# A Macaron block (top-k feed-forward, selective scan, feed-forward): the transposed gate moved from TensorE to VectorE and DRAM, softplus from one table, and a new issue order

## The chip, the cores and the metric

One core of one Trainium2 chip. The metric is the device time of one execution in microseconds (us), median of several runs. Five engines run their own instruction queues in order: PE (TensorE, matmuls), DVE (VectorE), ACT (ScalarE), POOL (GpSimd) and SP (SyncE, which in this kernel issues all DMAs). An instruction that waits on a semaphore holds everything behind it in its queue.

## The reference

`x` is [2, 2048, 1024] in float32. The block applies a feed-forward, a selective scan and the same feed-forward again:

```
x = x + 0.5 * ffn(layernorm(x))
x = x + ssm(layernorm(x))
x = x + 0.5 * ffn(layernorm(x))

ffn(x):  vecs   = A x                      # 64 experts a, rank 16 r
         arrows = norm(vecs over r)        # one number for each expert
         routes = one_hot(top4(arrows)).sum / 4
         v      = sum_a routes[a] vecs[a, r]
         return x W^T + bias + sum_{a, r} routes[a] v[r] B[a, :, r]

ssm(x):  delta_r, B, C = split(x Wx^T)
         delta = softplus(delta_r Wdt^T + b_dt)
         h_t   = exp(-delta exp(A_log)) h_{t-1} + delta B x      # 1024 channels, 16 states each
         return sum_n(h C) + x D
```

The last term of the feed-forward is a matrix product g B', where g[token, (r, a)] = v[token, r] * routes[token, a]. As the left operand of a matmul it is needed transposed, with (r, a) on the partitions: g^T.

## The kernel before, in words

The 4096 tokens are worked in 16 chunks of 256, two tiles of 128 tokens each. Each tile goes through the first feed-forward ("f"), a chunk then through the projections and softplus (`prepare`) and the scan (`scans`), and each tile through the second feed-forward ("g"). So there are 64 feed-forward tiles. For each, PE does three products of [128 x 1024] by [1024 x 1024]: `wa` (vecs), `ww` (x W^T) and `wb` (g B'). All three are issued at L578, 16 matmuls each, which the profile shows as 32 records since one float32 matmul is two.

Between the end of `wa` and the start of `wb` of the same tile lies the route chain: ACT squares vecs into `g` (`square`, L631); DVE sums the squares for each expert (L645), takes the top values (L648), marks them (L649) and turns the marks into 0.25 or 0 (L652); DVE multiplies vecs by the routes (`routed`, L658) and sums them into v (L668); POOL multiplies v by the routes into g (`spread`, L677, two halves); PE transposes g in eight blocks of 128 x 128 (`turn`, L560), ACT copies each half from PSUM to `gt` (L565), and `wb` reads `gt`. While that chain runs, PE works on `ww` of the same tile, which doesn't need it.

The scan keeps the channels replicated over partitions: SP fetches `rep` (delta and delta x, replicated 8 times by a broadcast read) from `du_d` in DRAM (L890), ACT makes the decay with Exp (L917), DVE makes the entry (L925) and scans (L932, two for each step), ACT saves the last state (L942), POOL multiplies by C (L945) and joins halves (L964), PE sums over states (L974), DVE adds the skip term (L988) and turns the result (L991), and SP stores and refetches it (`y_d`, `yt`, L385).

Softplus in `prepare` is made of six steps for each half of a chunk: ACT takes Abs and Relu of z + b (L806, L807), Exp of -|z| (L819), DVE three operations (L822, L827, L830), ACT Ln (L833), DVE one more (L836). Exp and Ln load different tables (ACT_TABLE_LOAD).

The order on every queue is not the order of the source. Each piece of work is a `Task` with an engine, a cost in us, a rank, the buffers that it takes and gives, and the tasks that it waits for. `Plan.order` runs a list schedule over these (an engine that is free takes the ready task of lowest rank whose buffers are free), and the instructions are emitted in the order of their planned starts. Costs, the latency from one engine to another (`HOP`) and the time in which a DMA lands stand in the `add` calls. The PSUM pool `bank` has five banks; `g`, `gt` have one buffer, `xnt` two, `rep` four.

Of the kernel before, what the change touches and what calls it, by code (L numbers as in the profile page):

```python
# [9 lines left out]
FP = mybir.dt.float32  # L30
AF = mybir.ActivationFunctionType
# [20 lines left out]

class Place:
# [10 lines left out]
class Task:  # L64
    __slots__ = (
        "eng", "cost", "emit", "rank", "take", "give", "port", "land", "turn", "waits", "users", "n",
        "at",
# [9 lines left out]
class Plan:  # L77
# [3 lines left out]
    HOP = 0.14  # L81
# [11 lines left out]
    def add(  # L93
        self, eng, cost, emit, reads=(), writes=(), rank=0.0, take=(), give=(), port=False, land=0.0,
        turn=None,
    ):
        t = Task()
        t.eng, t.cost, t.emit, t.rank = eng, cost, emit, rank
# [27 lines left out]
    def order(self):  # L126
# [7 lines left out]
        now = 0.0  # L134

        def arrive(t):
            heapq.heappush(ready[t.eng], (t.rank() if callable(t.rank) else t.rank, t.n))
# [5 lines left out]
        while True:  # L143
            moved = True
            while moved:
                moved = False
                for e in self.ENGINES:
# [34 lines left out]
                    end = now + t.cost  # L182
                    busy[e] = end
# [4 lines left out]
                    heapq.heappush(events, (end, t.n, 0))  # L188
# [7 lines left out]
            if kind == 0:  # L196
                if t.land:
                    heapq.heappush(events, (now + t.land, n, 1))
                else:
                    kind = 1  # L200
            if kind == 1:
# [4 lines left out]
                for u in t.users:  # L206
                    v = tasks[u]
                    v.waits -= 1
                    if v.waits == 0:
                        if v.eng == t.eng and not t.land:  # L210
                            arrive(v)
                        else:
                            heapq.heappush(events, (now + self.HOP, u, 2))
# [13 lines left out]
def macaron_kernel(  # L227
# [54 lines left out]
    places("stats", 6, [P, 17])  # L282
    places("choice", 2, [P, NA + len(PADS) + RANK])
# [4 lines left out]
    plan.pool("du_d", [dram.tile([D, 2, TC], FP, name=f"du_d{j}") for j in range(6)])  # L288
# [32 lines left out]
    pads = const.tile([P, len(PADS) + 1], FP, name="pads")  # L321
    less = pads[:, len(PADS) :]
    nc.gpsimd.memset(less, -1.5)
    for j, v in enumerate(PADS):
        nc.gpsimd.memset(pads[:, j : j + 1], v)

    marked = []
    for j in range(2):
        norms = const.tile([P, NA + len(PADS)], FP, name=f"norms_{j}")
        nc.gpsimd.tensor_copy(norms[:, NA:], pads[:, : len(PADS)])  # L330
        tops = const.tile([P, 2, 8], FP, name=f"tops_{j}")
        nc.gpsimd.tensor_copy(tops[:, 1, :TOPK], pads[:, :TOPK])
        marked.append((norms, tops))
    plan.pool("marked", marked)
# [10 lines left out]
    def load_rows(c, i):  # L345
# [16 lines left out]
        if c == 0:  # L362
            add("SP", 0.4, load_t, [], [(xt, 0), (xt, 1)], rank=-125.7 * n - 1008.5 if n else -2000.0,
                take=[xt], land=1.8)
            add("SP", 0.4, load, [], row(x_p), rank=121.5 * n - 1006.8, take=[x_p], land=1.4)
        else:
            add("SP", 0.8, emit, [], [(x_p, q) for q in range(KC)] + [(xt, 0), (xt, 1)],
                rank=n - (1006.5 if c == 1 else 100.0), take=[x_p, xt], land=5.5)

    def load_sum(c, i, rank):  # L370
# [5 lines left out]
        for g in range(2):  # L376
            yt = Place("yt")

            def fetch(g=g, yt=yt):
# [13 lines left out]
                take=[yt] if g else [x_p, yt], give=[y_d, x1_d], land=7.2)  # L393
# [13 lines left out]
    def load_all():  # L407
        def one(dst, src, key, us, rank):
            keys = [(*key, h) for h in range(2)] if isinstance(key, tuple) else [key]
            add("SP", us, lambda: nc.sync.dma_start(out=dst, in_=src), [], keys, rank=rank, land=3.6)  # L410

        def big(w_sb, w, name, rank):
# [10 lines left out]
            rank=-1000.0, take=[mean_w])  # L423
# [17 lines left out]
        for w_sb, name, key in ((wa, "wa", "pv"), (ww, "ww", "po")):  # L441
            total = Place("row" if name == "wa" else "delta")
            for k in range(1, KC):
                def gather(k=k, w_sb=w_sb, total=total):
# [5 lines left out]
                    take=[total] if k == 1 else [], port=True)  # L450
# [17 lines left out]
            for h in range(2):  # L468
# [10 lines left out]
                for k in range(KC):  # L479
# [4 lines left out]
                    add("DVE", 0.49, center, [(pt, 0)], [(name, k, h)], rank=-900.0, give=[pt])  # L484
# [6 lines left out]
            [], ["half_bias"], rank=272.6)  # L491
# [15 lines left out]
    def spread_of(x_p, st, factor, rank, after=()):  # L507
# [21 lines left out]
        def root():  # L529
            hv, r, t, q = (st.tile[:, j : j + 1] for j in (14, 15, 16, 12))  # L530
# [5 lines left out]
        add("DVE", 1.95, stats, row(x_p) + list(after), [(st, 0)], rank=-109.8 + rank, take=[st])  # L536
        add("ACT", 2.64, root, [(st, 0)], [(st, 1)], rank=72.4 + rank)

    def normalize(x_p, xn_p, rank, after=()):
# [4 lines left out]
        def scale():  # L544
            r, s = st.tile[:, 15:16], st.tile[:, 16:17]
# [6 lines left out]
    def turn(src, keys, dst, out_keys, rank, take=(), give_src=None):  # L552

        for g in range(2):
# [9 lines left out]
            def act(g=g, pt=pt):  # L564
# [4 lines left out]
                give=[src] if give_src else [])  # L569
# [510 lines left out]
```

## Time and profile before

| | us |
|---|---|
| median of 3 runs | 3112.06 (3110.25 to 3116.23) |
| span of the profiled execution | 3105.1 |
| PE busy | 3054.2 |
| ACT busy | 1869.4 |
| POOL busy | 2364.5 |
| mean granted TensorE clock | 0.998 |
| 16 DMA engines, share of the span that the dynamic queue's packets took | 52.6% |

The profile page comes from one execution. It gives for each engine the time in which it was busy, and for groups of equal instructions their count, total and mean time, the engine's idle time just before them and what ended that. Ends of matmuls are modelled, so the issue interval (from one start to the next, 0.432 us for a 128x512 float32 record) is the better measure of what a matmul costs. A window table gives the busy time by stretches of the span, a timeline the instructions in order of time.

### The profile page before, as it was taken

To read this page: it belongs to the slowest core of one execution; us is meant where nothing else is said; L and a number is where in the kernel's file an instruction comes from. 1 tells how busy PE (TensorE), PEld (TensorE's weight loads), DVE (VectorE), ACT (ScalarE), POOL (GpSimd) and SP (SyncE) were. 2 spreads that over 40 slices of the span, in tenths; PEclk is the share of its full clock that TensorE was granted. 3 is DMA by queue.
4 is the path that set the end of the run, shared out by engine and by line. 5 is a ranking of instruction groups with operands and counts; after the bars stand their busy time and mean duration, and the time that the engine had idled before them with its cause. 6 is when DMAs were issued, how large, how long until landed. Compare 5 with 4: busy or idle time off the path is not lost.

```text
span 3105.1 us, 36153 instructions
## 1 busy us (share of the span) xinstructions
PE 3054.2 (98%) x9020; PEld 1409.4 (45%) x9020; DVE 2816.7 (91%) x4683; ACT 1869.4 (60%) x4851; POOL 2364.5 (76%) x1882
## 2 busy tenths in 40 slices
PE   8999999999999999999999999999999999999999
PEld 3444444444444444444444444444444444444444
DVE  4279999999999999999999999999999999997951
ACT  1366666656666676666566665666557675565531
POOL 3148787888788788788887887878888788886861
PEclk9999999999999999999999999999999999999999
DMA  5154654646465465555555555555465555544630
GB/s 226 61 167 147 194 146 138 195 142 190 130 183 157 145 181 163 154 159 163 166 172 150 165 162 164 166 166 169 133 172 168 166 161 148 160 143 130 170 81 14
DMA packets 408371, 478.69 MB, mean 154 GB/s; under 512 B 161504, under 2 KB 253280, under 8 KB 408160
## 3 DMA queue, kind: packets, MB, share of 16 engines
q1 hardware_dynamic: 408160, 476.37, 52.6%
q8 instruction: 72, 1.18, 0.2%
q14 instruction: 139, 1.14, 0.1%
HBM read 375.07 MB, written 101.19 MB: 153 GB/s over the span
## 4 chain that ended last, share of the span: by engine, by line
PE 60%; DVE 24%; issue 6%; ACT 4%; DMA 2%; POOL 2%; SPq 0%; DVEq 0%; POOLq 0%; ACTq 0%
PE bank L578 53%; DVE h L932 10%; DVE h L925 5%; PE bank L974 2%; PE bank L560 2%; PE bank L748 1%; POOL h L945 1%; DVE g L658 1%; ACT da L917 1%; DVE norms L645 1%; PE bank L797 1%; DVE stats L512 1%; DMA rep<-du_d 1%; DVE choice L652 1%; DVE bank L988 1%
## 5 line engine op out<-in xcount | busy, mean ns | idle before, releaser
L945 POOL TENSOR_TENSOR h<-h,c 128x512 f32<-128x512 f32 x1024 | 1323.7, 1303 | 351.8 <-ACT state L942 316.8
L917 ACT ACTIVATE da<-rep,a_neg 128x256 f32<-128x256 f32 x2048 | 974.8, 477 | 725.4 <-DVE h L932 675.6
L932 DVE TENSOR_TENSOR_SCAN h<-da,state,h 128x256 f32<-128x256 f32 x2048 | 1404.8, 731 | 7.3 <-ACT da L917 5.5
L578 PE MATMUL bank<-wa,xnt 128*128 128x512 f32 x2048 | 905.6, 596 | 5.4 <-DVE wa L482 4.0
L578 PE MATMUL bank<-wb,gt 128*128 128x512 f32 x2048 | 895.9, 595 | 10.0 <-ACT gt L565 9.8
L578 PE MATMUL bank<-ww,xnt 128*128 128x512 f32 x2048 | 889.4, 592 | 0.0
L964 POOL TENSOR_TENSOR h<-h,h 128x512 f32<-128x512 f32 x512 | 654.7, 1279 | 40.1
L925 DVE TENSOR_TENSOR h<-rep,b 128x512 f32<-128x512 f32 x1024 | 670.2, 665 | 12.5 <-ACT b L879 6.7
L578 PEld LDWEIGHTS bank<-ww,xnt 128*128 128x128 f32 x2048 | 389.1, 190 | 489.8 <-issue 483.4
L578 PEld LDWEIGHTS bank<-wb,gt 128*128 128x128 f32 x2048 | 384.4, 190 | 485.2 <-issue 453.5
L578 PEld LDWEIGHTS bank<-wa,xnt 128*128 128x128 f32 x2048 | 384.9, 191 | 483.4 <-issue 470.8
L677 POOL TENSOR_TENSOR g<-choice 128x512 f32<-128x512 f32 x128 | 143.5, 1142 | 195.8 <-DVE choice L668 195.8
L942 ACT COPY state<-h 128x2 f32<-128x2 f32 x1024 | 187.9, 185 | 54.5 <-DVE h L932 53.3
L631 ACT ACTIVATE g<-bank 128x512 f32<-128x512 f32 x128 | 133.8, 1047 | 87.9 <-PE bank L578 55.6
L512 DVE BATCH_NORM_STATS2 stats<-xf 128x6 f32<-128x512 f32 x128 | 81.2, 676 | 57.4 <-DMA xf<-in_x 57.4
L616 POOL TENSOR_TENSOR xf<-xf,half_bias 128x512 f32<-128x512 f32 x64 | 81.1, 1287 | 66.4 <-DVE stats L512 66.3
L974 PE MATMUL bank<-h,summer 128*32 128x512 f32 x1024 | 123.1, 598 | 0.0
L645 DVE TENSOR_REDUCE norms<-g 128x64 f32<-128x1024 f32 x64 | 77.0, 1203 | 50.8 <-ACT g L631 49.4
L533 ACT ACTIVATE stats<-stats,pads 128x1 f32<-128x1 f32 x288 | 111.3, 387 | 9.7
L565 ACT COPY gt<-bank 128x512 f32<-128x512 f32 x128 | 71.4, 592 | 66.9 <-PE bank L560 66.4
L695 DVE SCALAR_TENSOR_TENSOR xg<-bank,stats,xg 128x512 f32<-128x512 f32 x64 | 47.4, 741 | 67.6 <-PE bank L578 67.2
L532 ACT ACTIVATE stats<-stats 128x1 f32<-128x1 f32 x288 | 58.1, 202 | 81.8 <-DVE stats L527 75.7
(84 smaller groups left out, 1969.2 us busy)
## 6 DMA issues: line engine op xcount, KB each, us to landing
rep<-du_d SPq DMA_DIRECT2D x1024, 256.0 KB, 3.7
xnt<-in_x_t SPq DMA_DIRECT2D x32, 512.0 KB, 4.1
xf<-in_x SPq DMA_DIRECT2D x32, 512.0 KB, 5.4
x_d<-xf SPq DMA_DIRECT2D x32, 512.0 KB, 3.3
u_d<-u SPq DMA_DIRECT2D x32, 512.0 KB, 4.7
ysb<-u_d SPq DMA_DIRECT2D x64, 256.0 KB, 3.4
du_d<-delta SPq DMA_DIRECT2D x32, 512.0 KB, 3.2
du_d<-u SPq DMA_DIRECT2D x32, 512.0 KB, 3.5
```

What stands on the lines that cost most here:

```text
L512: nc.vector.bn_stats(st.tile[:, 6 * s : 6 * s + 6], x_p.tile[:, s * HD : (s + 1) * HD])
L533: nc.scalar.activation(t, q, AF.Identity, bias=less, scale=hv)
L578: nc.tensor.matmul(ps[h].tile, lhsT=lhs.tile[:, k, :], rhs=w[:, k, h * HD : (h + 1) * HD], start=start and k == 0, stop=stop and k == KC - 1,)
L631: nc.scalar.activation(g_p.tile.rearrange("p (a r) -> p r a", r=RANK)[:, h * r2 : (h + 1) * r2, :], vecs(pv, h), AF.Square,)
L677: nc.gpsimd.tensor_mul(g_p.tile[:, h * HD : (h + 1) * HD].rearrange("p (r a) -> p r a", a=na), ch.tile[:, :NA].unsqueeze(1).to_broadcast([ ...
L917: nc.scalar.activation(da.tile[:, k, :], r.tile[:, k, 0, :], AF.Exp, scale=a_neg[:, q + k, j, hi : hi + 1],)
L925: nc.vector.tensor_mul(h.tile, r.tile[:, :, 1, :], bs[hi].tile.unsqueeze(1).to_broadcast([P, 2, TC]),)
L932: nc.vector.tensor_tensor_scan(h.tile[:, k, :], da.tile[:, k, :], h.tile[:, k, :], state[:, q + k, j, hi : hi + 1], ALU.mult, ALU.add,)
L942: nc.scalar.copy(state[:, q : q + 2, j, hi : hi + 1], h.tile[:, :, TC - 1 : TC])
L945: nc.gpsimd.tensor_mul(h.tile, h.tile, cs[hi].tile.unsqueeze(1).to_broadcast([P, 2, TC]))
L964: nc.gpsimd.tensor_add(first.tile, first.tile, h.tile)
L974: nc.tensor.matmul(y.tile[j // 2 * 2 * DB : (j // 2 + 1) * 2 * DB, :], lhsT=summer[:, DB * (1 - j % 2) : DB * (3 - j % 2)], rhs=sums[j].ti ...
```

## The change

Six things at once.

1. g is no longer formed in the token-major layout and transposed. DVE writes the 64 routes and the 16 sums v into one tile `rv` [128 x 96], turns it in 32 x 32 blocks (`transpose`), and SP writes it to DRAM as `rv_d` [96 x 128] with four DMAs (`put_rv`, runs of 128 bytes). SP then fetches it with four more (`fetch_rv`): the routes twice into `rt` [128 x 128], and the sums as rows of 4 KB, each broadcast to 64 partitions, into `gt`. POOL multiplies `gt` by `rt` in place (`spread`). The transposes on PE and the copies on ACT for g are gone. The columns of `wa` are laid out in another order on the host to suit.
2. The marks become 0.25 or 0 in one ACT instruction (`mark`, Relu with scale -0.25 and bias -1) in place of one on DVE.
3. Softplus is ACT's own function, four calls for each half of a chunk; Abs, Relu, Exp, Ln and four DVE operations are gone.
4. `du_d` is laid out so that one `rep` fetch is one DMA with rows of 4 KB, in place of two with rows of 2 KB.
5. The planner's costs are replaced by a table of durations (`TIMES`), its DMAs get an issue time, a service time on one shared lane and a landing time (`MOVES`), hops differ by engine, a wait within an engine costs something too, and a table load on ACT costs 1.28. Every kind of task gets a constant added to its rank (`SHIFT`).
6. Pools: `rv`, `rvt`, `rt` with one buffer each and `rv_d` with three come, `choice` and `marked` go, `stats` loses one of six. The two banks that one half's softplus reads are taken together.

```diff
+SHIFT = {
+    "load_t": -2251.4,
+    "load": -5612.6,
+    "load_w": 2052.3,
...
+    "products wa": 709.3,
...
+    "put_rv f": -1786.5,
+    "fetch_rv f": 480.6,
+    "spread f": -238.0,
+    "products ww": -50.3,
+    "products wb": -1364.2,
...
+MOVES = {
...
+    "fetch": (0.62, 1.37, 2.3),
...
+    "put_rv f": (1.65, 0.65, 2.0),
+    "fetch_rv f": (2.4, 1.8, 2.5),
...
-    HOP = 0.14
+    HOP = {"PE": 0.22, "DVE": 0.12, "ACT": 0.12, "POOL": 0.1, "SP": 0.05}
+    SAME = {"PE": 0.0, "DVE": 0.17, "ACT": 0.1, "POOL": 0.12, "SP": 0.0}
+    TABLE = 1.28
...
-    places("choice", 2, [P, NA + len(PADS) + RANK])
+    places("rv", 1, [P, NA + 32])
+    places("rvt", 1, [P, NA + 32])
+    places("rt", 1, [P, P])
+    plan.pool("rv_d", [dram.tile([NA + 32, P], FP, name=f"rv_d{j}") for j in range(3)])
...
-    plan.pool("du_d", [dram.tile([D, 2, TC], FP, name=f"du_d{j}") for j in range(6)])
+    plan.pool("du_d", [dram.tile([P, KC, 2, TC], FP, name=f"du_d{j}") for j in range(6)])
...
-            nc.vector.tensor_scalar(routes, routes, CHOSEN, 1.0 / TOPK, ALU.is_equal, ALU.mult)
+        def mark():
+            nc.scalar.activation(
+                rv.tile[:, :NA], rv.tile[:, :NA], AF.Relu, bias=less_one, scale=-1.0 / TOPK
+            )
...
         def total():
             nc.vector.tensor_reduce(
-                ch.tile[:, NA + len(PADS) :],
+                rv.tile[:, NA : NA + RANK],
                 g_p.tile.rearrange("p (r a) -> p r a", a=na), AX.X, ALU.add,
             )
+            nc.vector.transpose(rvt.tile, rv.tile)
...
+        def put_rv():
+            for b in range(P // 32):
+                nc.sync.dma_start(
+                    out=rv_d.tile[:, 32 * b : 32 * b + 32].rearrange("(m i) j -> i m j", i=32),
+                    in_=rvt.tile[32 * b : 32 * b + 32, :].rearrange("p (m j) -> p m j", j=32),
+                )
+
+        def fetch_rv():
+            for h in range(P // NA):
+                nc.sync.dma_start(out=rt.tile[h * NA : (h + 1) * NA, :], in_=rv_d.tile[:NA, :])
+            vs = rv_d.tile[NA : NA + RANK, :].rearrange("(h c) t -> h (c t)", h=P // NA)
+            for h in range(P // NA):
+                nc.sync.dma_start(
+                    out=gt.tile[h * NA : (h + 1) * NA, :, :].rearrange("p c t -> p (c t)"),
+                    in_=vs[h].unsqueeze(0).to_broadcast([NA, KC * P]),
+                )
...
             def spread(h=h):
-                v0 = NA + len(PADS) + h * r2
+                part = gt.tile[:, h * HC : (h + 1) * HC, :]
                 nc.gpsimd.tensor_mul(
-                    g_p.tile[:, h * HD : (h + 1) * HD].rearrange("p (r a) -> p r a", a=na),
-                    ch.tile[:, :NA].unsqueeze(1).to_broadcast([P, r2, NA]),
-                    ch.tile[:, v0 : v0 + r2].unsqueeze(2).to_broadcast([P, r2, NA]),
-                )
-
-            add("POOL", 0.99, spread, [(ch, 0), (ch, 1)], [(g_p, h)], rank=-27.7 + rank, port=True,
-                give=[ch])
-        turn(g_p, lambda g: [(g_p, g)], lambda g: gt.tile[:, g * HC : (g + 1) * HC, :],
-             lambda g: [(gt, g)], rank, take=[gt], give_src=True)
+                    part, part, rt.tile.unsqueeze(1).to_broadcast([P, HC, P])
+                )
...
+            def softplus(g=g, pts=pts, dg=dg):
+                for k in range(HC):
+                    nc.scalar.activation(
+                        dg.tile[:, k, :], pts[k // 2].tile[:, k % 2 * TC : (k % 2 + 1) * TC],
+                        AF.Softplus, bias=bdt[:, g * HC + k : g * HC + k + 1],
+                    )
...
                 def fetch(q=q, j=j, r=reps[j]):
-                    for k in range(2):
-                        d0 = (q + k) * P + j * DB
-                        rows = du_d.tile[d0 : d0 + DB, :, :].rearrange("d s t -> d (s t)")
-                        nc.sync.dma_start(
-                            out=r.tile[:, k, :, :].rearrange("p s t -> p (s t)"),
-                            in_=rows.unsqueeze(1).to_broadcast([DB, LO, 2 * TC]),
-                        )
+                    rows = du_d.tile[j * DB : (j + 1) * DB, q : q + 2, :, :]
+                    nc.sync.dma_start(
+                        out=r.tile.rearrange("p k s t -> p (k s t)"),
+                        in_=rows.rearrange("d k s t -> d (k s t)").unsqueeze(1).to_broadcast(
+                            [DB, LO, 4 * TC]
+                        ),
+                    )
```

## The prediction

> **What bounds the kernel now.** I read the page's busy times first, then the busy times by windows of the span, then the groups of instructions with the idle time before each, and last the timeline of one tile.
>
> ```profile
> span 3105.1 us, 36153 instructions
> PE 3054.2 (98%) x9020; PEld 1409.4 (45%) x9020; DVE 2816.7 (91%) x4683; ACT 1869.4 (60%) x4851; POOL 2364.5 (76%) x1882
> ```
>
> ```profile
> 800.00:1200.00 400.00, 397.45 (x1183) 183.42 (x1182) 390.86 (x648) 260.92 (x673) 327.86 (x259) 1.00 0.56 163
> 2950.00:3050.00 100.00, 97.55 (x275) 43.62 (x274) 52.01 (x94) 33.74 (x91) 51.67 (x43) 1.00 0.24 63
> 3050.00:3105.00 55.00, 50.36 (x126) 22.53 (x124) 7.45 (x12) 3.73 (x5) 3.31 (x3) 1.00 0.05 19
> ```
>
> Columns of the windows: stretch, length, busy PE, PEld, DVE, ACT, POOL, granted clock, DMA share, GB/s. In the middle PE (397 of 400) and DVE (391 of 400) are both nearly full; in the last 155 us DVE empties and PE stays full. PE is idle for 51 us of 3105 in all, 14 of them in the first 60 us. So PE sets the end, and DVE is close behind it.
>
> ```profile
> L578 PE MATMUL bank<-wb,gt 128*128 128x512 f32 x2048 | 895.9, 595 | 10.0 <-ACT gt L565 9.8
> L560 PE MATMUL bank<-ident,g 128*128 128x128 f32 x512 | 73.3, 276 | 14.8 <-ACT state L942 3.6 <-ACT u L565 3.6 <-ACT xnt L565 3.0
> ```
>
> These two groups hold what the present route chain costs PE: the transposes, and 14.8 + 10.0 = 24.8 us in which PE stood idle before a transpose of g or before `wb`.
>
> **Removed from PE.** Ends of matmuls are modelled, so I price by starts:
>
> ```profile
> 1848.49 1.04 PE L560 MATMUL bank<-ident,xg 128*128 128x128 f32 x8
> 1849.36 0.60 PE L560 MATMUL bank<-ident,g 128*128 128x128 f32 x4
> 1849.80 1.10 PE L797 MATMUL bank<-part,wdt 128*128 128x256 f32 x4
> ```
>
> Eight transposes take 0.87 us from start to start, four 0.44. 64 tiles x 8 x 0.1095 = **-56.1 us**. The 73.3 us of the group is the other bound; it counts overlap with neighbours, so I take 56.1. The waits around them go too: **-24.8 us**.
>
> **Removed elsewhere, costed at nothing.** DVE loses the four softplus steps (44.7 + 24.6 + 40.1 + 42.2 = 151.6 us) and the marks (42.9), and gains 64 turns of 96 columns: L991 turns 512 in 0.716 us, so between 0.13 in proportion and 0.72; I take 0.25, 16 us. Net -178. ACT loses the g copies (71.4), Abs, Relu, Exp and Ln (60.4 + 61.0 + 33.6 + 33.8), and gains 128 softplus calls at the 0.476 us of L807 (61) and 64 marks at 0.19 (L942) to 0.39 (L533). Its loads of tables stay: the changed order holds 61 where 65 were. None of this is on PE; it shows only as slack. Were PE to get much faster, DVE's 2817 - 178 = 2639 would still lie 390 us below.
>
> **The new chain.** What counts is how long `wb` must wait after `wa` of its tile, and how much other work PE has meanwhile. The chain, from a tile near the end where little else runs:
>
> ```profile
> 3028.57 3.60 PE L578 MATMUL bank<-ww,xnt 128*128 128x512 f32 x8
> 3029.83 1.22 DVE L645 TENSOR_REDUCE norms<-g 128x64 f32<-128x1024 f32 x1 [14.93 <-ACT g L631]
> 3031.68 0.20 DVE L652 TENSOR_SCALAR choice<-choice 128x68 f32<-128x68 f32 x1
> 3033.30 1.22 DVE L668 TENSOR_REDUCE choice<-g 128x16 f32<-128x1024 f32 x1
> 3034.66 2.04 POOL L677 TENSOR_TENSOR g<-choice 128x512 f32<-128x512 f32 x2 [11.18 <-DVE choice L668]
> ```
>
> `wa` ends where `ww` starts, 3028.57; the sums end at 3034.52: 5.95 us. From there:
> - Without the old mark (-0.20), with a trip to ACT and back (0.19 to 0.39, and two hops of 0.03 to 0.14) and the turn (0.13 to 0.72): 6.2 to 7.2. I take 6.5.
> - `put_rv` is four DMAs. Three issues ahead of the last, 0.34 (stores of `bc_d`) to 0.51 (four fetches of `yt` in 2.04): 1.0 to 1.5. Then the landing, 1.5 (least, `bc_d`) to 3.1 (its median). 2.5 to 4.6; I take 3.4.
> - `fetch_rv`, four more that wait for that landing: 3 x 0.51 to 0.59, then 1.8 (least, `yt`) to 3.7 (median, `rep`, the same 256 KB as a `gt` half). 3.3 to 5.5; I take 4.4.
> - One half of `spread`, 1.02 to 1.29 with its hops: 1.4 to 1.6.
>
> ```profile
> DMA to landing us min/median/max: 1.5/3.1/6.0
> DMA to landing us min/median/max: 1.8/3.5/6.7
> rep<-du_d SPq DMA_DIRECT2D x1024, 256.0 KB, 3.7
> ```
>
> The first line is of `bc_d`, the second of `yt`. Sum: 13.4 to 18.9 us, taken 15.8, when nothing else runs. In the middle other work stands between the steps. By the changed kernel's instruction order, DVE has 1.2 us of scan work between choose and `routed` (0.5 of it hidden by the mark's trip) and 1.0 between `routed` and the sums, on average, at the trace's 0.6 for an entry and 1.31 for two scans; POOL can be inside a 1.3 us operation. That adds 1.2 to 3.5, taken 2.4. **Chain in the middle: 14.6 to 22.4, taken 18.2.** The old chain was about 11: 5.95, 2.2 for `spread`, 1.5 or so for transposes and copies.
>
> *A rule against the change.* The Trainium skill's page "DMA: Bandwidth & Descriptors" (Bandwidth) says that transfers under 64 KB are dominated by descriptors, and its section "Anatomy of one DMA" gives about 2.0 us fixed for each DMA plus bytes over 436 GB/s, fitted for another issuing path. By it the two landings would be an estimated 2.0 and 2.6 us, the quiet chain an estimated 15.0 and the sum below some 8 us smaller. The medians here (3.1 to 3.7) lie above that fit, the least (1.5, 1.8) below.
>
> **The cover.** I took the changed kernel's order on PE, gave each instruction the trace's issue interval, and added up what stands between the last `wa` and the first `wb` of each tile. Before: median 16.2 us, least 14.7. After: median 20.1, mean 20.7; 11 tiles have less than 18.2, and the last four have 15.7, 18.2, 14.7 and 13.8. The order now puts a part of the next tile's `wa` or a scan's sum ahead of `wb`. PE's issue intervals sum to 3026 us before and 2970 after, which is the 56 again.
>
> Exposed time, the sum over tiles of chain minus cover where positive: at 18.2 in the first 60 tiles 11 us, at 15.8 in the last four 3. Chains scatter as their landings do (1.5 to 6.0): at 16.2 and 20.2 the first 60 give 0 and 47, mean 23. I take **+25**; ends 0 (at 14.6) and 145 (132 at 22.4 and 13 at 18.9 in the last four).
>
> **Queues that the steps pass.** On SP, `fetch_rv` holds all behind it until `put_rv` has landed; most often that is two `rep` fetches, on which ACT's decay and DVE's entry wait. `rep` has four buffers of about 4 us of DVE work each, against some 6 us of blockade (3.4, then four issues): nothing, or a few us for DVE, which has them. SP's issues: 512 fewer for `rep` at 0.54, 512 more at 0.34 to 0.59. DMA volume grows by 64 x 624 KB, 40 on 479 MB, at a queue share of 53%. On ACT decays stand behind a mark that waits for DVE, for the 0.1 of a hop.
>
> At the start both `xf` loads (1 MB) now precede `xnt`, for which PE waits 4.5 us at the beginning; at the 275 GB/s of the first 60 us that is up to **+4**, taken whole.
>
> **Sum.** 3105.1 - 56.1 - 24.8 + 25 + 4 = 3053. The median of the runs lies 7 above the profiled execution: **3060**.
>
> **Rivals.**
> - *Chain longer than its cover* (slower). If small DMAs next to the `rep` traffic land at their medians or later and DVE's queue adds its 3.5, the chain is 22.4: 3105 - 81 + 145 + 4 + 7 = **3180**. It decides from exposed time of 77 us, a chain of about 21. For it: the maxima of 6.0 and 6.7, and that the whole gain is only 1.2 us a tile. Against: the cover grew by 4, and PE being late shortens the queueing of the others.
> - *Chain wholly hidden.* Exposed 0 to 5: **3037**. For it: the least landings. Against: the last tiles' cover of 13.8.
> - *SP's blockade starves the scan*: DVE would have to lose over 6 us a tile (390 / 64) before it decides; then some **3120**. DVE waited 5 us for `rep` in the whole run.
> - *Gain given back*: exposed about 77, **3112**.
>
> **Chances.** Within 0.2% (6 us) nothing can be told from no change here. Partly exposed, 3037 to 3100 (itself 3040 to 3090): 0.50. Wholly hidden: 0.13. Longer than the cover: 0.28. Starved: 0.03. Given back: 0.06. So faster 0.63, same 0.06, slower 0.31. The range goes from 3030 to 3155: below it lies 0.05, above it about half of the slow case, 0.14.
>
> **What would show it.** Right: no L560 group for g, PE busy near 2998, and idle before `wb` of about 25 us put down to POOL's `gt`, most of it at tiles with little cover. Put to fetch landing together near 8 us. Wrong: idle before `wb` over 80; `yt`-sized landings above 4; DVE or ACT waiting on `rep`; more than 61 table loads; or PE waiting before `wa` because a route holds the banks longer.

## The result, and the profile after

| | before | after |
|---|---|---|
| median of the runs, us | 3111.15 (3108.60 to 3116.23) | 3125.01 (3121.18 to 3134.92) |
| span of the profiled execution | 3105.1 | 3119.4 |
| PE busy / PE idle in that span | 3054.2 / 50.9 | 3014.3 / 105.1 |
| PE's issue intervals, summed over its instructions | 3026 | 2970 |
| mean granted clock | 0.998 | 0.992 |

The changed kernel is slower by half a per cent: ratio 1.0048, 95% interval 1.003 to 1.0067. The transposes did leave PE, and more than their worth came back as waiting.

The page of the changed kernel, its busy times:

```profile
span 3119.4 us, 34436 instructions
PE 3014.3 (97%) x8508; PEld 1360.4 (44%) x8508; DVE 2647.6 (85%) x4556; ACT 1728.1 (55%) x4591; POOL 2327.4 (75%) x1881
```

The same kernel by windows (columns as in the prediction):

```profile
800.00:1200.00 400.00, 386.25 (x1131) 176.31 (x1130) 359.69 (x618) 243.05 (x644) 314.63 (x253) 0.99 0.61 172
2950.00:3050.00 100.00, 98.93 (x253) 43.74 (x252) 23.45 (x49) 16.33 (x39) 21.21 (x17) 1.00 0.21 51
```

Before, PE was busy 397 of the 400 us that begin at 800; now 386, with DVE at 360 instead of 391. In the 100 us from 2950 PE is nearly full (98.9), and the last four tiles, where the prediction feared the smallest cover, wait 4.9 us for `wb` together (0.6, 0, 1.6 and 2.7). So most of the loss is spread over the middle. Three groups of the changed kernel with the idle time before them, then two of them before the change:

```profile
L700 PE MATMUL bank<-wa,xnt 128*128 128x512 f32 x2048 | 908.0, 596 | 13.3 <-ACT xnt L686 13.1
L700 PE MATMUL bank<-wb,gt 128*128 128x512 f32 x2048 | 907.4, 601 | 50.3 <-POOL gt L829 50.2
L681 PE MATMUL bank<-ident,row 128*128 128x128 f32 x256 | 34.7, 278 | 9.9 <-ACT row L668 9.9
```
```profile
L578 PE MATMUL bank<-wa,xnt 128*128 128x512 f32 x2048 | 905.6, 596 | 5.4 <-DVE wa L482 4.0 <-ACT xnt L565 1.4
L560 PE MATMUL bank<-ident,row 128*128 128x128 f32 x256 | 33.8, 275 | 0.0
```

Idle time before `wb` rose from 10.0 to 50.3; the 14.8 before the transposes of g went; the waits before `wa` rose by 7.9, before the transposes of `row` by 9.9, before the softplus products by 5.8, at the start by 3.9, the rest by about 1. That is 54 us more idle. PE's busy time fell by 40 where the issue intervals fell by 56: 16 us are matmuls that ran more slowly. 54 + 16 - 56 = 14, the difference of the spans. The record of the granted clock accounts for the 16: it stood at half for 51 us of the changed kernel and for 14 us before, and half of the time in which PE was busy there is 22 against 6 us.

The longest wait before `wb` in the timeline of the changed kernel shows both losses (start, length, engine, line, operation; in brackets the idle time before it):

```profile
2627.83 1.19 DVE L796 TENSOR_REDUCE rv<-g 128x16 f32<-128x1024 f32 x1
2629.06 0.28 DVE L800 STREAM_TRANSPOSE rvt<-rv 128x96 f32<-128x96 f32 x1
2629.37 1.73 SPq L807 DMA_DIRECT2D rv_d<-rvt  x4
2632.93 1.11 SPq L814 DMA_DIRECT2D rt<-rv_d  x2
2633.03 1.04 PE L681 MATMUL bank<-ident,xg 128*128 128x128 f32 x8
2634.15 1.18 SPq L817 DMA_DIRECT2D gt<-rv_d  x2
2638.93 2.50 POOL L829 TENSOR_TENSOR gt<-gt,rt 128x512 f32<-128x512 f32 x2 [3.30 <-DMA gt<-rv_d]
2640.25 10.21 PE L700 MATMUL bank<-wb,gt 128*128 128x512 f32 x17 [6.18 <-POOL gt L829]
2641.26 0.34 PEld L700 LDWEIGHTS bank<-wb,gt 128*128 128x128 f32 x1 [0.52 <-issue]
2646.43 0.19 PEld L700 LDWEIGHTS bank<-wb,gt 128*128 128x128 f32 x1 [0.24 <-issue]
```

The turn ends at 2629.34, the puts take until 2631.1 to issue, the fetches start at 2632.93, and the second `gt` fetch is issued at about 2634.7 and seen by POOL at 2638.93. PE finished its cover (the `xg` transposes) at 2634.07 and waited 6.18 us. Then weight loads come every 0.86 us (0.34 + 0.52) until 2645.5, and every 0.43 (0.19 + 0.24) after: PE ran at half speed for 5.3 us. The windows view shows it in the granted clock, the third column from the right:

```profile
2630.00:2640.00 10.00, 4.07 (x16) 2.08 (x14) 9.83 (x20) 6.61 (x19) 4.01 (x4) 0.94 0.68 176
2640.00:2650.00 10.00, 9.75 (x17) 4.26 (x18) 5.31 (x9) 3.44 (x11) 10.00 (x10) 0.72 0.52 152
```

Last, the DMA issues of the changed kernel (KB each, median us to landing):

```profile
rep<-du_d SPq DMA_DIRECT2D x512, 512.0 KB, 4.9
gt<-rv_d SPq DMA_DIRECT2D x128, 256.0 KB, 4.1
rv_d<-rvt SPq DMA_DIRECT2D x256, 12.0 KB, 1.5
rt<-rv_d SPq DMA_DIRECT2D x128, 32.0 KB, 3.2
```

The put lands quickly, in 1.5. The fetch of `gt` takes 4.1 in the median.

### The profile page after: what moved, and what is told of

The parts are those of the page before. It is cut to its first block, busy times and chain, and to the rows that moved or that the text cites. A ratio compares the mean times of both kernels' runs of the same rounds, so it can differ in the third digit from the quotient of the medians.

```text
span 3119.4 us, 34436 instructions
## 1 busy us (share of the span) xinstructions
PE 3014.3 (97%) x8508; PEld 1360.4 (44%) x8508; DVE 2647.6 (85%) x4556; ACT 1728.1 (55%) x4591; POOL 2327.4 (75%) x1881
## 4 chain that ended last, share of the span: by engine, by line
PE 45%; DVE 24%; DMA 11%; issue 7%; ACT 5%; POOL 4%; SPq 3%; POOLq 0%; DVEq 0%; ACTq 0%
PE bank L700 41%; DVE h L1045 12%; DVE h L1038 4%; DMA gt<-rv_d 3%; DMA xf<-in_x 3%; ACT da L1030 2%; DVE stats L631 1%; PE bank L1087 1%; POOL h L1077 1%; DVE g L786 1%; DVE rv L796 1%; DMA rv_d<-rvt 1%; POOL h L1058 1%; DVE norms L767 1%; POOL gt L829 1%
## 5 line engine op out<-in xcount | busy, mean ns | idle before, releaser
L1058 POOL TENSOR_TENSOR h<-h,c 128x512 f32<-128x512 f32 x1024 | 1288.5, 1277 | 368.8 <-ACT state L1055 275.0
L1045 DVE TENSOR_TENSOR_SCAN h<-da,state,h 128x256 f32<-128x256 f32 x2048 | 1379.8, 730 | 7.3 <-ACT da L1030 4.6
L700 PE MATMUL bank<-wb,gt 128*128 128x512 f32 x2048 | 907.4, 601 | 50.3 <-POOL gt L829 50.2
L700 PE MATMUL bank<-wa,xnt 128*128 128x512 f32 x2048 | 908.0, 596 | 13.3 <-ACT xnt L686 13.1
L700 PE MATMUL bank<-ww,xnt 128*128 128x512 f32 x2048 | 901.4, 595 | 0.8 <-DVE ysb L1104 0.2
L1038 DVE TENSOR_TENSOR h<-rep,b 128x512 f32<-128x512 f32 x1024 | 651.4, 672 | 33.4 <-ACT b L993 18.0
L700 PEld LDWEIGHTS bank<-wb,gt 128*128 128x128 f32 x2048 | 390.7, 192 | 553.2 <-issue 473.5
L829 POOL TENSOR_TENSOR gt<-gt,rt 128x512 f32<-128x512 f32 x128 | 159.9, 1269 | 221.4 <-DMA gt<-rv_d 220.6
L1055 ACT COPY state<-h 128x2 f32<-128x2 f32 x1024 | 172.2, 181 | 2.1 <-DVE h L1045 2.1
L516 POOL TENSOR_TENSOR xg<-yt,xg 128x512 f32<-128x512 f32 x64 | 82.0, 1282 | 47.0 <-DMA yt<-y_d 46.2
```

Of the source, the lines that this page charges most:

```text
L700: nc.tensor.matmul(ps[h].tile, lhsT=lhs.tile[:, k, :], rhs=w[:, k, h * HD : (h + 1) * HD], start=start and k == 0, stop=stop and k == KC - 1,)
L829: nc.gpsimd.tensor_mul(part, part, rt.tile.unsqueeze(1).to_broadcast([P, HC, P]))
L1038: nc.vector.tensor_mul(h.tile, r.tile[:, :, 1, :], bs[hi].tile.unsqueeze(1).to_broadcast([P, 2, TC]),)
L1045: nc.vector.tensor_tensor_scan(h.tile[:, k, :], da.tile[:, k, :], h.tile[:, k, :], state[:, q + k, j, hi : hi + 1], ALU.mult, ALU.add,)
L1055: nc.scalar.copy(state[:, q : q + 2, j, hi : hi + 1], h.tile[:, :, TC - 1 : TC])
L1058: nc.gpsimd.tensor_mul(h.tile, h.tile, cs[hi].tile.unsqueeze(1).to_broadcast([P, 2, TC]))
```

## The experiments

The first theory (A): the chain through DRAM is longer than its cover, and the clock adds to it. The rival (B): the new order loses the time elsewhere. "Chain" below is the time from the start of the second half of `square` to the end of the first half of `spread`, measured on all 64 tiles in the timeline (this starts later than the prediction's chain, which starts at the end of `wa`: by 1.6 us in the mean of the changed kernel); "cover" is the PE work that stands between a tile's last `wa` and first `wb`.

**turn_back: only the route of g^T undone.** POOL spreads g, PE transposes it and ACT copies it as before; softplus, the long `rep` rows and the new planner stay.

```diff
-        add("SP", 1.7, put_rv, [(rvt, 0)], [(rv_d, 0)], ...
-        add("SP", 1.2, fetch_rv, [(rv_d, 0)], [(rt, 0), (gt, 0), (gt, 1)], ...
+        turn(g_p, lambda g: [(g_p, g)], lambda g: gt.tile[:, g * HC : (g + 1) * HC, :], ...
```

> The changed kernel with the old route chain: POOL's spread makes g, PE turns it, ACT copies it, no DRAM; softplus from its table, long rep rows and the new planner stay (the order is another one, since the tasks differ). Theory A (the DRAM chain costs what it saves): PE's issue sum goes back to 3026, the wait before wb to about 25 us with the transposes, 3095 to 3115. Theory B (the new planner's order is at fault): over 3120, with waits before other products.

Measured: 3099.42, ratio 0.9961 (0.9948 to 0.9974). Its page and its group for `wb`:

```profile
span 3099.4 us, 34695 instructions
PE 3049.7 (98%) x9020; PEld 1409.1 (45%) x9020; DVE 2627.2 (85%) x4493; ACT 1785.9 (58%) x4717; POOL 2297.9 (74%) x1881
```
```profile
L698 PE MATMUL bank<-wb,gt 128*128 128x512 f32 x2048 | 895.7, 595 | 5.5 <-ACT gt L684 5.5
```

The other five parts together, in this order, are worth 12 us of gain; the route by DRAM loses 26 us against PE's transposes under the same planner, although it takes 56 us of issue off PE. The two orders differ, since the tasks do, and the constants were searched with the DRAM route in place.

**fewer, and nowait on top of it: eight DMAs made five.** `put_rv` is three DMAs, `fetch_rv` two (one for `gt`, written 2 x 64 x 1024, one for `rt`); every order stays. nowait then also reads rows of an input instead of `rv_d`, so that the fetch need not wait for the put.

```diff
-            for h in range(P // NA):
-                nc.sync.dma_start(out=gt.tile[h * NA : (h + 1) * NA, :, :]..., in_=vs[h]...)
+            nc.sync.dma_start(
+                out=gt.tile.rearrange("p c t -> p (c t)"),
+                in_=vs.unsqueeze(1).to_broadcast([P // NA, NA, KC * P]),
+            )
```

> The changed kernel with the order on every queue as it is, but put_rv as three DMAs instead of four and fetch_rv as two instead of four, gt's first. By the changed kernel's trace an issue of put_rv takes 0.43 us and one of fetch_rv 0.59, and gt's landing is counted from its own issue, so the chain from wa to wb gets about 1.4 to 2.2 us shorter. Theory A (the route chain is longer than PE's other work, and a long wait lowers the granted clock after it): taking 1.7 off each of the changed kernel's 32 waits before wb leaves 14 of their 50 us, and most stretches of low clock go with them: 3125 - 36 - 10 = about 3080. Theory B (the new order loses its time elsewhere, in waits that only move when one is taken away): 3115 or more, with PE idle as much as before in other groups.

> As the kernel with fewer DMAs, but fetch_rv reads rows of an input of the same size in place of rv_d, so it doesn't wait for put_rv's landing (1.9 us in the median, 2.5 in the mean). It leaves out that the routes reach the product, put_rv is still written. Together about 4.4 us off the chain. Theory A: 2 of the 50 us before wb are left, the clock stays at 0.997 or above, 3125 - 48 - 15 = about 3062. Theory B: 3100 or more.

Measured: fewer 3867.41 (1.243, 1.2412 to 1.2449) and nowait 3820.41 (1.2281, 1.2263 to 1.23). Both expectations missed by more than 750 us: the one `gt` transfer lands some 17 us after its issue, and the chain's mean goes from 20.5 to 31.7. As a larger dose of the same trouble the run is still of use: 11.2 us more chain on 64 tiles are 716 us, of which 634 show as more idle time before `wb` (683.8), and PE's busy time rises by 135 at a granted clock of 0.90. That is both halves of theory A, on a large scale. Why the transfer landed so late is answered below (narrow, wide2).

**more: `fetch_rv` as eight half-size DMAs.**

```diff
+                for g in range(2):
+                    nc.sync.dma_start(
+                        out=gt.tile[h * NA : (h + 1) * NA, g * HC : (g + 1) * HC, :]...,
```

> The changed kernel with the order as it is, but fetch_rv as eight DMAs of half the size, so that the last lands four issues, about 2.4 us, later. Theory A: each of the 32 waits before wb grows by up to 2.4, and tiles that had a little to spare join them: wait before wb 50 to about 130 us, a few more stretches of low clock, 3125 + 80 + 15 = about 3220. Theory B: under 3150, since the waits would stand in for others.

Measured: 3155.07 (1.0135, 1.0119 to 1.0152), idle before `wb` 59.4, chain mean 20.6. The time lies between the two expectations. Four more issues cost less than expected: halves of 128 KB land in 3.1 us instead of 4.1 (medians), so the chain hardly grew. Of the 30 us lost, 9 are before `wb`; the rest is in other waits and in the clock.

**gt_first, and nowait2 on top of it.** gt_first issues the two large `gt` fetches ahead of the two small ones of `rt`. nowait2 again fetches input rows of the same shapes, without the wait for the put.

```diff
+            for h in range(P // NA):
+                nc.sync.dma_start(out=gt.tile[h * NA : ...
             for h in range(P // NA):
                 nc.sync.dma_start(out=rt.tile[h * NA : ...
-            for h in range(P // NA):
-                nc.sync.dma_start(out=gt.tile[h * NA : ...
```

> The changed kernel with the order of all work as it is, but the four DMAs of fetch_rv swapped: gt's two first, rt's two after them. In the changed kernel's trace a gt DMA lands 4.1 us after its issue and an rt DMA 3.2, so the last landing comes about 0.9 us sooner. Theory A (chain over cover): 0.9 off each of the 32 waits before wb leaves 27 of 50 us, and the stretches of low clock get fewer: about 3095. Theory B (other waits of the new order): 3115 to 3125. The kernel with one gt DMA said nothing on this, since that DMA took 17 us.

> As the kernel with gt first, but fetch_rv reads rows of an input of the same size, in the same four shapes, in place of rv_d, so it doesn't wait for put_rv to land. It leaves out that the routes reach the product. From the first issue of put_rv to the first of fetch_rv it is 3.2 us now and four issues, 1.7, then: 1.5 us less, 2.4 with the swap. Theory A: 8 of 50 us of waits before wb are left and the granted clock is back at 0.997: about 3070. Theory B: 3110 or more, PE's other idle time growing.

Measured: gt_first 3106.98 (0.9992, 0.9982 to 1.0002), idle before `wb` 42.4; nowait2 3098.79 (0.9971, 0.9956 to 0.9985), idle 40.2. Both times lie between what theory A and theory B expected. nowait2 leaves out that the routes reach the product. Without the wait, put to fetch falls from 3.4 to 2.5 us, but the landings of `gt` go from 4.6 to 5.4 in the median: what is issued sooner takes longer to land. So a third theory (C): a fetch lands when the bytes ahead of it and its own have been moved.

**half_bytes: gt_first, with each `gt` fetch moving half its row.** The kernel leaves out the other half of g; a tile fetches 256 KB less.

```diff
-                    out=gt.tile[h * NA : (h + 1) * NA, :, :].rearrange("p c t -> p (c t)"),
-                    in_=vs[h].unsqueeze(0).to_broadcast([NA, KC * P]),
+                    out=gt.tile[h * NA : (h + 1) * NA, :HC, :].rearrange("p c t -> p (c t)"),
+                    in_=vs[h, :HD].unsqueeze(0).to_broadcast([NA, HD]),
```

> The kernel with gt first, but each gt DMA fetches half of its row (128 KB for 256), the order of all work as it is. It leaves out half of the gate, whose place stays zero. In the runs so far gt landed later the sooner it was issued (4.1, 4.6, 5.4 us in the median). If that landing is the time until the DMA engines have moved what lies ahead of it and its own bytes (theory C), 288 KB less at some 170 to 240 GB/s bring it and rt some 1.1 us forward, the wait before wb falls from 42 to about 20 us and the time by 25 to about 3080. If it is a fixed latency, landing and time stay within 0.3 us and 8 us of the kernel with gt first (3107).

Measured: 3071.69 (0.986, 0.9841 to 0.988), landing median 3.7, idle before `wb` 21.7. The groups and landings of gt_first, then of half_bytes:

```profile
L700 PE MATMUL bank<-wb,gt 128*128 128x512 f32 x2048 | 904.4, 599 | 42.4 <-POOL gt L829 42.2
gt<-rv_d SPq DMA_DIRECT2D x128, 256.0 KB, 4.6
```
```profile
L702 PE MATMUL bank<-wb,gt 128*128 128x512 f32 x2048 | 900.8, 598 | 21.7 <-POOL gt L831 21.7
gt<-rv_d SPq DMA_DIRECT2D x128, 128.0 KB, 3.7
```

Half of the bytes of `gt` is worth 35 us here, by about 1 us of chain. A fixed latency is ruled out: a fetch's own bytes count for when it lands. That the bytes ahead of it count too is suggested by nowait2, and not tested alone.

**short_rep: the `rep` fetch again as two DMAs with rows of 2 KB.**

```diff
+                    for k in range(2):
+                        rows = du_d.tile[j * DB : (j + 1) * DB, q + k, :, :]
```

> The changed kernel with each rep fetch as two DMAs with rows of 2 KB, as it was before the change; layout of du_d and order of all work stay. SP issues 512 more DMAs of 0.54 us, and some stand ahead of put_rv or fetch_rv. If the long rows matter for the chain (theory C, in which rep traffic ahead of gt sets its landing), the wait before wb grows by 10 us or more and the time to 3140 or over. If they matter little: 3115 to 3135.

Measured: 3137.89 (1.0067, 1.0045 to 1.0089) against 1.0048 (1.003 to 1.0067) for the change: the intervals overlap, so the long rows are worth somewhere from nothing to some 20 us. Idle before `wb` is 50.7 (50.3 in the change) and the landing of `gt` 4.0 (4.1): twice the number of `rep` DMAs, for the same bytes, does not reach the chain.

**plan_dram and plan_turn: the planner told what was measured.** The change's table lets a `gt` fetch land 2.5 us after its issue, `bc` 2.2, `rep` 2.3. Both kernels get longer times, set by the traces (4.5, 3.5, 3.3 and so on), and an equal search of the rank constants; plan_dram from gt_first, plan_turn from turn_back. So each differs from its parent in two things, the times and the search, which were not tried apart.

```diff
-    "fetch": (0.62, 1.37, 2.3),
+    "fetch": (0.62, 1.37, 3.3),
-    "fetch_rv f": (2.4, 1.8, 2.5),
+    "fetch_rv f": (2.4, 1.8, 4.5),
```

> The kernel with gt first, with the planner told what the trace shows (put_rv lands 3.1 us after its first issue, fetch_rv 6.3, xf, yt, y_d, rep and the stores about 1 later than it had them, a product 3.46 for 3.43) and its rank constants searched anew; between the last wa and the first wb PE now has 21.3 us of other work on average for 20.7. Theory A: the DRAM chain can be covered when its true length is planned for: wait before wb under 25 us, clock 0.995 or better, 3060 to 3085, faster than before and than the old chain under the same treatment less some 10. Theory B (the route through DRAM can't pay, since landings vary by more than the cover): wait over 35 us, 3095 or more.

> The kernel with the old route chain (transposes on PE), softplus from its table and long rep rows, with the same landing times told to the planner and as long a search of its rank constants: the control of the run above. PE's issue sum is 3026 us, 56 more. With some 40 us of idle time: 3080 to 3100. Theory A wants it above the run with the planned DRAM chain, theory B at or below it.

Measured: plan_dram 3085.53 (0.9915, 0.9892 to 0.9938), plan_turn 3054.99 (0.9816, 0.9801 to 0.983). The page of plan_turn and its group for `wb`:

```profile
span 3052.5 us, 34308 instructions
PE 3035.8 (99%) x9020; PEld 1406.8 (46%) x9020; DVE 2620.0 (86%) x4493; ACT 1781.1 (58%) x4717; POOL 2309.6 (76%) x1881
```
```profile
L699 PE MATMUL bank<-wb,gt 128*128 128x512 f32 x2048 | 903.2, 594 | 0.9 <-ACT gt L685 0.9
```

PE is idle for 17 us of 3052: this order is within 27 us of its issue sum of 3026. It is the fastest kernel of the study, with all 512 transposes on PE. Theory A had expected it behind plan_dram; it is 30 us ahead. plan_dram itself lies at the edge of what theory A expected, with 28.0 us idle before `wb` where under 25 was expected.

**narrow and wide2: one `gt` fetch of 512 KB in two shapes.** Both are gt_first with the two `gt` fetches made one. narrow writes it 2 x 64 x 1024 (the two halves outermost). wide2 writes it 64 x 2 x 1024 (the experts outermost), with the rows of `wb`'s weights and of `rt` put in that order. (The "wide" that narrow's expectation speaks of is wide2's shape.)

```diff
-            # narrow
-                in_=vs.unsqueeze(1).to_broadcast([P // NA, NA, KC * P]),
+            # wide2
+                in_=vs.unsqueeze(0).to_broadcast([NA, P // NA, KC * P]),
```

> The same one DMA of 512 KB written with the two halves as the outermost dimension (2 x 64 x 1024), all else as in wide. Theory D: lands in 16 to 18 us, chain some 11 us longer than in gt_first, idle before wb 600 to 700, granted clock near 0.90, time 3750 to 3870. Rival (the slow landing came from the other edits of that run, the three puts or the doubled rt): lands as in wide, 3090 to 3130.

> The run called narrow answered one half: with the four puts and the two rt fetches as in gt_first, a single fetch of gt written 2 x 64 x 1024 alone makes the time 3819 (one run, 3109 before beside it), idle before wb 640, granted clock 0.907. Here the same 512 KB are one DMA written 64 x 2 x 1024: partition p holds expert p // 2 and half p % 2, the two fetches of rt and the rows of the wb weights are put in that order, all else as in gt_first (time 3107, idle before wb 42). Theory D (the outermost dimension says over how many DMA engines a transfer is spread): lands like a rep fetch of the same size, 5 to 6 us, one issue fewer, idle before wb 30 to 55, time 3090 to 3120. Rival (one DMA of 512 KB out of these few rows is slow in any order, since 128 descriptors read the same two rows of 4 KB): idle before wb 600 to 700, time 3750 to 3870.

Measured: narrow 3819.27 in its one run (3109.28 before, beside it), wide2 3081.26 (0.9913, 0.9885 to 0.9941). A wait in the windows of narrow, then the same two groups, narrow's and wide2's, and wide2's landing:

```profile
1010.00:1020.00 10.00, 0.00 (x0) 0.00 (x0) 1.34 (x3) 2.17 (x7) 0.98 (x1) 0.58 0.52 133
1020.00:1030.00 10.00, 9.66 (x17) 4.28 (x18) 5.68 (x13) 4.65 (x15) 10.00 (x9) 0.73 0.23 71
```
```profile
L700 PE MATMUL bank<-wb,gt 128*128 128x512 f32 x2048 | 1038.8, 671 | 640.5 <-POOL gt L828 640.5
```
```profile
L700 PE MATMUL bank<-wb,gt 128*128 128x512 f32 x2048 | 902.0, 598 | 28.2 <-POOL gt L833 28.0
```
```profile
gt<-rv_d SPq DMA_DIRECT2D x64, 512.0 KB, 4.9
```

The same bytes in the same number of DMAs give `spread` its start 5.8 us after the issue in the median (least 3.9) with 64 outermost, and after 17.4 (least 12.7) with 2 outermost. The last tile's fetch, when little else moves, shows why; the last two columns are the DMA share, of 16 engines, and GB/s (narrow, then wide2):

```profile
3790.00:3794.00 4.00, 0.00 (x0) 0.00 (x0) 0.00 (x0) 0.00 (x0) 0.00 (x0) 0.51 0.13 53
```
```profile
3055.20:3056.80 1.60, 1.60 (x5) 0.71 (x4) 0.00 (x0) 0.00 (x0) 0.00 (x0) 1.00 0.89 334
```

With 2 outermost, 0.13 of 16 engines is two engines at work, at 53 GB/s; with 64 outermost it is 14 of them, at 334 GB/s. The Trainium skill's page "DMA: Bandwidth & Descriptors" (Why a DMA increments its semaphore by 16 and not by 1) states the rule: a copy goes to the largest number of engines up to 16 that divides the outermost size of both sides. For an outermost 2 that gives two engines, as the trace shows.

**wide_plan and plan_wide: that shape in the order of plan_dram, and with the planner told of it.** wide_plan changes only the shape; plan_wide also tells the planner (1.8 to issue, 4.3 to land) and searches on for 50 minutes.

```diff
-    "fetch_rv f": (2.4, 1.8, 4.5),
+    "fetch_rv f": (1.8, 1.8, 4.3),
```

> plan_dram with one thing changed: gt fetched by one DMA written 64 x 2 x 1024, as in wide2 (its planner still told the landing times of two fetches, so every order is plan_dram's, 3085.53). From gt_first to wide2 the same change took 25.7 us and 14.2 of the idle time before wb (42.4 to 28.2). Theory (the chain's length against its cover sets what is lost): plan_dram has 28.0 idle before wb left, so 10 to 18 off that, 3060 to 3078. Rival (what is lost in plan_dram lies in its other waits, 22.2 before wa and 18.9 before the xg transposes, that the fetch doesn't touch): 3079 to 3086. Against the turn on PE under the same landing times, 3054.99: theory and rival both leave the DRAM route behind.

> The same kernel with the planner told of the shape (fetch_rv 1.8 to issue and 4.3 to land in place of 2.4 and 4.5) and its constants searched on from plan_dram's for 50 minutes more; the planner's own end is 3049.5. Theory: a shorter chain that the planner knows of leaves some 10 to 20 us of idle time before wb and the waits for copies, 3055 to 3080, so the DRAM route ends level with the turn on PE (3055) or up to 25 behind it. Rival (the DRAM route is itself better once its transfer is spread well, since PE has 56 us less to issue): under 3045.

Measured: wide_plan 3084.72 (0.9925, 0.9907 to 0.9942), no different from plan_dram: its idle before `wb` fell from 28.0 to 21.5, the time did not follow, as the rival had it. plan_wide 3078.18 (0.9897, 0.988 to 0.9913). Its groups:

```profile
L700 PE MATMUL bank<-wa,xnt 128*128 128x512 f32 x2048 | 917.2, 600 | 32.9 <-ACT xnt L686 21.7 <-ACT u L686 4.6 <-DVE xf L847 3.6
L700 PE MATMUL bank<-wb,gt 128*128 128x512 f32 x2048 | 895.4, 594 | 13.0 <-POOL gt L833 12.9
L681 PE MATMUL bank<-ident,xg 128*128 128x128 f32 x256 | 36.6, 278 | 13.4 <-ACT u L686 10.7 <-POOL xg L516 1.7 <-ACT xnt L686 0.5
```

Only 13 us are left before `wb`; 46 stand before `wa` and the `xg` transposes, where PE waits for copies by ACT and for work of other tiles. The DRAM route ends 23 us behind PE's transposes, although its constants were searched for longer.

Side by side (medians):

| route of g^T | planner of the change | traced landing times, new search |
|---|---|---|
| DRAM, `rt` first (the change) | 3125.01 | |
| DRAM, `gt` first | 3106.98 | 3085.53 |
| DRAM, one `gt` fetch, 64 outermost | 3081.26 | 3078.18 (3084.72 not replanned) |
| transposes on PE | 3099.42 | **3054.99** |

## Why the prediction was wrong, step by step

The mechanism named, a chain through DRAM that is only partly covered, was the one that decided. Its length was taken too short, and two terms were missing.

- *PE, -56.1:* as predicted, 3026 to 2970 by issue intervals.
- *DVE and ACT, nothing:* right for the work removed and added. A turn of 96 columns took 0.278 us (0.25 taken), a mark 0.346 (0.19 to 0.39), a softplus call 0.473 (0.476 taken). DVE did not wait for `rep`, and SP's blockade starved nothing.
- *Start, +4:* 3.9.
- *The cover:* right. Taken as 20.7 us in the mean with 13.8 at the last tile, it was 21.1 and 13.9 in the trace.
- *The chain, "taken 18.2":* this is the step that failed. From the end of `wa`, where the prediction starts it, it measured 22.1 us in the mean (median 21.5).

| term, us | taken | least in 64 tiles | mean |
|---|---|---|---|
| from the end of `wa` to the first put, with other work on ACT and DVE | 6.5 + 2.4 | 6.4 | 10.2 |
| `put_rv`, first issue to the first issue of `fetch_rv` | 3.4 | 2.9 | 3.8 |
| `fetch_rv`, first issue to the start of `spread` | 4.4 | 5.8 | 6.8 |
| `spread`, one half | 1.5 | 1.3 | 1.3 |

The fetch was mis-sized most, by 2.4 us a tile: no tile did it in the 4.4 taken. The prediction took 1.8 to 3.7 us of landing, from `yt` and from the `rep` fetches of before. From the issue of the second `gt` fetch to `spread` it took at least 4.0, with the two `rt` fetches and the first `gt` fetch ahead of it; half_bytes showed that the bytes count. The first row is 1.3 over: the second half of `square` starts 1.6 us after the end of `wa` in the mean (least 0.2), mostly because ACT is still in other work, the decays above all; the sum left that out. The prediction's estimate of 2.0 and 2.6 us for the two landings, which its sum did not use, compares with medians of 1.5 and 4.1; its quiet chain of 15.0 comes out only with the least issue times that it lists.

- *The price of the chain, +25 where 50 came:* ten kernels of one order show how steep it is (chain as in the experiments, from `square`):

| same order, same cover | chain, mean us | idle before `wb` |
|---|---|---|
| half_bytes | 19.2 | 21.7 |
| wide2 | 19.6 | 28.2 |
| nowait2 | 20.0 | 40.2 |
| gt_first | 20.1 | 42.4 |
| after | 20.5 | 50.3 |
| short_rep | 20.6 | 50.7 |
| more | 20.6 | 59.4 |
| nowait | 30.9 | 638.2 |
| narrow | 31.0 | 640.5 |
| fewer | 31.7 | 683.8 |

1.2 us of chain, from half_bytes to the change, are 29 us of idle time, so the fetch's 2.4 alone are enough for the missing 25. The prediction's own curve would not have given 50: it sets one length against the cover of every tile, and by that rule 22.1 us leave some 125 us exposed (an estimate from the traced covers). In the trace long chains stand on tiles with long cover (correlation 0.92), presumably since the same other work lengthens both. That the curve has 47 us at 20.2 is luck: a chain too short and a price too high.

- *Missing: the clock, +16.* A long wait costs twice. The wait shown above lost 6.2 us and then about 2.6 (half of 5.3).
- *Missing: PE's other waits, +25 beyond the start's 4.* The sum took it that removing work from PE leaves its neighbours where they are. turn_back's waits before `wa` (6.8) and `row` (5.1) are smaller than the change's (13.3 and 9.9). half_bytes, with the change's order and 29 us less before `wb`, still waits 13.2 before `wa`, but 4.5 before `row`: the first comes with the order, half of the second with the late `wb`.
- *Sum:* 3053 + 25 (more before `wb`) + 16 + 25 = 3119, against a span of 3119.4.
- *Rivals:* of the four, "gain given back" came nearest by its time, "longer than its cover" by its mechanism. The latter had the length right (22.4) and its price wrong (145 us exposed against 50). Its turning point was put at 77 us of exposed time; with clock and neighbours it lies near 40. At gt_first's 42 the time is 0.9992 of before.
- *Signs:* the idle time before `wb` came out between the sign of right (25) and that of wrong (over 80); put to landing took 10.6 us in the mean, where about 8 stood for right; the landings of `yt` were at the limit of 4 (median 4.0).

What stays open: the softplus table and the long `rep` rows were not tried one by one against before, and each search of the planner's constants is one search: part of the 23 us between plan_wide and plan_turn may be its luck. How much of the gain of plan_dram and plan_turn comes from the landing times and how much from the search is open too.

## What to carry to other kernels

Price a transfer that others precede by its bytes and the issues ahead of it, not by the median landing of a like one, and look at its outermost dimension: 64 there kept 14 of 16 engines busy, 2 kept two. Where one engine is full and a chain nearly fills its cover, half a microsecond of chain for each tile decides. Start the chain where its first engine may be late, and set chain against cover tile by tile, not one length against all. And try the planner before the move: with longer landing times and a new search, the untouched transposes gained 44 us, most of the 52 that the whole change was forecast to bring.

## What the runs showed of the hardware

- The granted clock falls by a grid of time slots, not by the length of a wait. In each trace the stretches at half clock start on one grid of 3.413 us: in the changed kernel at 614.68, 676.12, 843.37 and 996.97, which are 18, 49 and 45 slots apart. What counts is the idle share of one slot (by the profile's ends of matmuls, which are modelled). A wait of 2.05 us before `wb` (2919.28 to 2921.33) lay within one slot and left PE busy for 1.36 of 3.41 us; the next slot ran at half clock. A wait of 3.21 us (1302.67 to 1305.88) was split over two slots, with 1.91 and 1.70 us busy, and the clock stayed whole:

```profile
2918.68:2922.09 3.41, 1.36 (x8) 0.85 (x7) 3.41 (x6) 2.34 (x6) 2.08 (x2) 1.00 1.00 259
2922.09:2925.50 3.41, 3.41 (x5) 1.35 (x4) 3.41 (x7) 1.85 (x6) 3.41 (x4) 0.50 0.50 144
1300.76:1304.17 3.41, 1.91 (x8) 0.88 (x6) 3.31 (x9) 1.97 (x8) 3.14 (x3) 1.00 0.90 231
1304.17:1307.58 3.41, 1.70 (x5) 0.81 (x6) 3.41 (x7) 3.25 (x10) 3.41 (x4) 1.00 0.87 225
1307.58:1311.00 3.42, 3.42 (x9) 1.51 (x9) 3.42 (x6) 2.42 (x7) 3.42 (x4) 1.00 0.63 163
```

The 16 traces of this case hold some 14,300 such slots at full clock. None with PE idle for less than 53% of it was followed by half clock, and every one with more than 59% was. So waits from 1.8 us up can cost twice, as they happen to lie in the grid.

The Trainium skill's page "TensorE: Matmul & The Clock Gate" (Part 1: The HAM clock gate) has the clock fall to half after an idle window of about 3.4 us that runs free of the program. The half speed (0.86 against 0.43 us from one weight load to the next) and the grid of 3.413 us agree; that the slot has to be idle as a whole does not, since 60% was enough above.

- Two DMAs of 256 KB with 64 outermost and one of 512 KB with 64 outermost land at nearly the same time (medians 4.6 and 4.9 us); with 2 outermost the wait from issue to `spread` is three times as long (17.4 against 5.8).
